# Two transformer blocks on one core: second head pairs, norm rows, first cross-attention scores and a dispatch moved

## The chip, the cores and the metric

The kernel runs on one core of a Trainium2 chip. A core has five engines, each with its own instruction queue: TensorE (PE, matrix products and transpositions, written to PSUM), VectorE (DVE), ScalarE (ACT), GpSimd (POOL) and SyncE (SP, which issues most of the DMA transfers). PSUM has eight banks of 128 x 512 values in float32. Times are microseconds on the device, from a median of several runs; the profile is of one execution.

## The reference

Two transformer blocks follow each other on x of shape (2, 1024, 256), with 16 heads of 16. Block 0 adds self-attention, then cross-attention to 64 context rows, then a mixture of 8 experts of which every row takes two. Block 1 adds self-attention, cross-attention to the same 64 rows (a mask adds 0 or -10000 to the scores), then a dense feed-forward layer. Each step is normed first.

```python
# block 0
q = ln(x);  x = x + mha(q, q, sa)                 # softmax(q k' / 4) v per head
x = x + mha(ln(x), ln(ctx), ca)                   # 64 keys
h = ln(x);  vals, idx = top_k(h @ rw.T + rb, 2)
gates = softmax(vals)
x = x + sum_k gates[k] * (gelu(h @ fc1[idx[k]].T + b1) @ fc2[idx[k]].T + b2)
# block 1
q, k, v = split(ln(x) @ qkv.T);  x = x + softmax(q k' / 4) v @ sa_proj.T
bias = (1 - mask) * -10000
x = x + softmax(ln(x) @ q_w.T (ctx @ k_w.T)' / 4 + bias) (ctx @ v_w.T) @ ca_proj.T
x = x + gelu(ln(x) @ fc1.T + b1) @ fc2.T + b2
```

## The kernel before

The 2048 rows of x lie in SBUF (x_sb, 16 tiles of 128 rows) and are worked on in four units of 512 rows, numbered 0 to 3: batch b = 0 or 1, and half qh = 0 or 1 of its queries.

**Cells.** Each block's self-attention is cut into 128 cells. A cell computes four tiles of 128 x 512 transposed scores (line L969), which ACT turns into exponentials (L947, tile pt_s) and PE multiplies with the values (L1024); ten cells ahead (LEAD = 10) the scores of other four tiles are computed for their row maxima, which DVE reduces (L937). The planner counts 3.3 us for a cell (CELL). From cell 118 on no maxima are left: a flag, maxima[0], turns False. The flag also says which engine helps: helper() is POOL while it is True and DVE afterwards.

**Fillers.** Everything else is a generator (a task) whose yields tell the planner what has been issued: a positive yield is PE time, a negative one is a wait in microseconds before the task may go on. In the cells a wait counts at least one whole cell. A light task advances once a cell by rank; others fill what PE time is left. After the last cell `Stream.rest` plays the tasks that remain, by rank, on a planned clock on which waits count as they are written. What comes out is a fixed order of instructions on each engine, which the engines then run in that order.

**Self-attention's end.** A unit has four groups of four heads, eight cells each (h = 4 * unit + g). When a group's parts are summed (L1037 on POOL, or DVE after cell 118), `finish` sends rows and sums out through DRAM (L538, L539); at the second group of a pair it gathers them (L543), inverts the sums (L554), sends them back (turn_out, L558), spreads them over partitions (spread_out, L562) and divides (L568); each step has its own cell. For a unit's second pair (g == 3, that is h = 3, 7, 11, 15) the projection of the unit (L492, tile ot_s) follows, added to x by DVE (L500). The very last pair of groups goes by L880, L886, L894 and L901 instead.

**Cross-attention of a unit.** Statistics (L398, L399) and inverse roots (L381 to L389, fourteen small operations) of the norm, its rows (xn_c, L412) and their transpositions (L424); the queries (L1295); the scores in `weigh` (L1337, on the tiles q_c and kbd), whose row maxima DVE reduces from PSUM (L1345, tile mx_c); maxima split in two parts (L1358, L1359) and transposed (L1364); scores again, transposed, with the maxima subtracted (L1374, L1380), exponentials (L1385), value products (L1434) and sums (L1444), reciprocals (L1453), division (L1459, L1466) and the projection (L492, tile q_c). In `weigh` the sixteen heads are two groups g of eight; the four rows r of a group are pairs of heads, with 32 of the 128 partitions each. Units 0 and 1 start while maxima[0] is True and go by a finer plan (the `whole` path), units 2 and 3 by the list of steps in the diff. In block 1 each score tile begins with a product that writes the mask (L1324).

**Dispatch of a unit (block 0).** Norm again (st_m, root_m, rows xd_m L1568, transpositions L424), router products (L1581), the top two (L1604 to L1613, the tile hot_m), counts (L1621 to L1642), places and gates (L1647 to L1668), and eight scatters of rows into a DRAM buffer sorted by expert (POOL, L1676). When dispatch 1 has counted, `find(2)` looks up which experts have full tiles (L1689 to L1802); then rows (xs, L1856) and expert weights (L1864) are loaded. An expert slot of 256 rows transposes xs (L1926), turns who and gates (L1932 to L1949), and runs both layers (L1961, L1992) before its results are scattered (L2007). Later slots wait for dispatches 2 and 3. Slots run on after the cells of block 0 and beside the beginning of block 1.

**Block 1's end.** After its cells, the feed-forward layers of units (L2145, L2157) run, with cross-attention of units 2 and 3 between.

PSUM banks come from a list of free ones, in the order in which they were given back; a product waits for whoever used the bank before.

Of the kernel before, what the change touches and what calls it, by code (L numbers as in the profile page):

```python
# [235 lines left out]
def two_blocks(  # L236
# [27 lines left out]
    def bank():  # L264


        i = free.pop(0)
        return i, banks[:, i, :]
# [10 lines left out]
    weights = {}  # L279
# [58 lines left out]
    def choice(layer, pool):  # L338
        for b in range(1 + layer):
            chosen[layer].append(pool.tile([P, 2, P], F32R, name=f"chosen{layer}{b}"))  # L340
# [26 lines left out]
    maxima = [True]  # L367
# [23 lines left out]
    def statistics(src, nt, tag, pool=small, each=False, engine=None):  # L391


        st = pool.tile([P, 8, 6], F32, tag="st", name=f"st_{tag}", bufs=4)
        mv = pool.tile([P, 8, 2], F32, tag="mv", name=f"mv_{tag}", bufs=6)
        rs = pool.tile([P, 8], F32, tag="rs", name=f"rs_{tag}", bufs=6)
        for t in range(nt):
            nc.vector.bn_stats(st[:, t, :], src(t))  # L398
            nc.vector.bn_aggr(mv[:, t, :], st[:, t, :])  # L399
            if each or t % 2 == 1:  # L400
                yield -1.2
        inverse_roots(rs[:, :nt], mv[:, :nt, 1], tag, pool, engine or helper())
        yield -3.4 if engine is None else -4.4
        return mv, rs

    def center(src, pair, held, tag, pool=small):
# [174 lines left out]
    def self_attention(layer, tail, heads, arrive, extra, when_ready, beside=None):  # L581
# [259 lines left out]
        def finish(h, cell):  # L841


            b, qh, g = h // 8, h // 4 % 2, h % 4
            if g == 0:
                ot[b, qh] = opool.tile([P, 2, 512], F32, tag="ot", name=f"ot_{names}{b}{qh}")
            if layer == 0 and h >= 8 * B - 2:

                if g == 3:
                    stream.add(  # L850
                        side_by_side([acc.pop(h - 1), acc.pop(h)], ot[b, qh][:, 1, :]), 2.0,
                        mark="compact", rank=80,
                    )
                    project(b, qh, ["compact"])
                return
            if g % 2 == 0:
                sm = small.tile([P, 32], F32, tag="sums", name=f"sums_{names}{h}")
                sums[g // 2] = next_heads(), sm
            n, sm = sums[g // 2]
            dst = ot[b, qh][:, g // 2, :]  # L860
            send(acc.pop(h), n, g % 2, sm)
            if g % 2 == 1:
                by = opool.tile([P, 512], F32, tag="by", name=f"by_{names}{h}", bufs=1)
                gather(n, dst)
                slow = maxima[0]
                at_cell(cell + 1, lambda: invert(n, sm))
                at_cell(cell + 1 + slow, lambda: turn_out(n, sm))
                at_cell(cell + 2 + slow, lambda: spread_out(n, by))

                late = 3 + 2 * slow  # L870
                at_cell(cell + late, lambda: divide(dst, by))
                if g == 3:
                    at_cell(cell + late + 1, lambda: project(b, qh))
# [434 lines left out]
    def weigh(layer, b, pool, w, name, held):  # L1308
# [7 lines left out]
        mx = pool.tile([P, 2, 4, 4, 2], F32, tag="mxc", name=f"mx_{name}")  # L1316
        turned_mx = []

        def scores(g, n, t0=0, nt=4):

            got = [(r, *bank()) for r in (2 * n, 2 * n + 1)]
            for r, _, p in got if layer == 1 else ():
                at = slice(32 * r, 32 * r + 1)
                nc.tensor.matmul(  # L1324
                    p[:, : nt * P].rearrange("p (c k) -> p c k", k=SK),
                    lhsT=ones[at, :].bitcast(F32R),
                    rhs=mask_f[at, b * SK : (b + 1) * SK]
                    .bitcast(F32R)
                    .unsqueeze(1)
                    .to_broadcast([1, 2 * nt, SK]),  # L1330
                    start=True,
                    stop=False,
                )
            for t in range(nt):
                for r, _, p in got:
                    rows = slice(32 * r, 32 * r + 32)
                    nc.tensor.matmul(  # L1337
                        p[:, t * P : (t + 1) * P],
                        lhsT=q[rows, g, (t0 + t) * P : (t0 + t + 1) * P],
                        rhs=kbd[rows, g, b].rearrange("p u k -> p (u k)"),  # L1340
                        start=layer == 0,
                        stop=layer == 0 or t == nt - 1,
                    )
            for r, i, p in got:
                nc.vector.tensor_reduce(  # L1345
                    mx[:, g, r, t0 : t0 + nt, :].rearrange("p t u -> p (t u)"),
                    p[:, : nt * P].rearrange("p (c k) -> p c k", k=SK),
                    AX.X, ALU.max, negate=True,
                )
                free.append(i)  # L1350
# [120 lines left out]
        if whole:  # L1471
# [2 lines left out]
            cells = [[] for _ in range(22)]  # L1474
            for k in range(8):
                g, n, half = k // 4, k // 2 % 2, k % 2
                cells[k].append((scores, g, n, 2 * half, 2))
                if k % 4 == 3:
                    cells[k].append((parts, g))
            cells[9].append((largest,))  # L1480
# [14 lines left out]
                elif now is not cells[-1]:  # L1495
                    yield 0.0
            return
        costs = {scores: 1.0 + extra, largest: 0.9, weights: 1.2, undivided: 1.9, division: 0.55}
        rs = range(4)
        for step, *args, wait in (  # L1500
            (scores, 0, 0, None),
            (scores, 0, 1, None),
            (parts, 0, None),
            (scores, 1, 0, None),
            (scores, 1, 1, None),
            (parts, 1, -1.8),
            (largest, -0.8),
            (weights, 0, rs, -1.6),
            (undivided, 0, None),
            (weights, 1, rs, -1.6),  # L1510
            (division, 0, None),
            (undivided, 1, None),
        ):
            step(*args)
            if step in costs:
                yield costs[step]
            if wait:
                yield wait
# [36 lines left out]
    def dispatch_task(unit, pool, counted):  # L1555
# [46 lines left out]
        for k in range(2):  # L1602
# [4 lines left out]
            first = small.tile([P, 4], F32, tag="first", name=f"first_{name}{k}")  # L1607
            nc.vector.tensor_reduce(first, hot, AX.X, ALU.max)
            nc.vector.tensor_tensor(hot, desc_b, first.unsqueeze(2).to_broadcast(shape), ALU.is_equal)
            yield -1.0  # L1610
            if k == 0:
                nc.vector.scalar_tensor_tensor(lg, hot, -3.0e38, lg, ALU.mult, ALU.add)
                nc.vector.tensor_scalar(  # L1613
# [51 lines left out]
        for k in range(2):  # L1665
            mine = small.tile([P, 4, E], F32, tag="mine", name=f"mine_{name}{k}")
            nc.vector.tensor_tensor(mine, hots[k], place.rearrange("p e t -> p t e"), ALU.mult)
            nc.vector.tensor_reduce(at[:, k, :], mine, AX.X, ALU.max)  # L1668
            yield -0.5
        counted()  # L1670

        for t in range(4):
# [133 lines left out]
    class Mixture:  # L1806
# [211 lines left out]
        def find(self, units):  # L2018
# [9 lines left out]

                caps = [self.caps[last], *expert_tiles(f"{units}", (OVER, ANY) if last else (FULL,))]
            yield -0.9  # L2030
            pool = self.epool[1] if self.epool else const
            places = Places()
            yield from places.make(pool, f"{units}", n, had, caps, last)
            self.places.append(places)
# [146 lines left out]
    def block(layer, tail, heads=None, beside=None):  # L2181
# [8 lines left out]
        if layer == 0:  # L2190
            open_pools()
            context_places(0, pools["cpool"])
            choice(0, pools["cpool"])
            bias_out.extend(pools["dpool"].tile([P, D], F32, name=f"bias_out{i}") for i in range(2))
        made, ys, ready = [], [], {}

# [310 lines left out]
```

## Time and profile before

| what | us |
|---|---|
| three runs | 1526.99, 1522.6, 1530.24 |
| median | 1526.99 |
| profiled execution | 1523.92 |
| its span | 1522.0 |
| PE busy in it | 1439.3 |
| DVE busy | 982.7 |
| ACT busy | 919.9 |
| POOL busy | 355.3 |
| mean granted PE clock | 0.986 |

A line of the page reads: engine, busy time, share of the span, instructions. A line of a timeline reads: start, length, engine, line of the kernel, operation, output <- inputs, tile sizes, how many instructions were joined, and in brackets how long the engine had been idle before and what released it. A line of the table of stretches reads: from:to, length, busy time of PE, of its weight loads, of DVE, ACT and POOL (with the number of instructions), granted PE clock, share of the DMA engines' time, GB/s. In the profile, block 0's cells end at 543.8 us and what the rest of block 0 and the beginning of block 1 share follows.

### The profile page before, as it was taken

To read this page: it belongs to the slowest core of one execution; us is meant where nothing else is said; L and a number is where in the kernel's file an instruction comes from. 1 tells how busy PE (TensorE), PEld (TensorE's weight loads), DVE (VectorE), ACT (ScalarE), POOL (GpSimd) and SP (SyncE) were. 2 spreads that over 40 slices of the span, in tenths; PEclk is the share of its full clock that TensorE was granted. 3 is DMA by queue.
4 is the path that set the end of the run, shared out by engine and by line. 5 is a ranking of instruction groups with operands and counts; after the bars stand their busy time and mean duration, and the time that the engine had idled before them with its cause. 6 is when DMAs were issued, how large, how long until landed. Compare 5 with 4: busy or idle time off the path is not lost. (4 is left out here: it accounts for less than half of the span.)

```text
span 1522.0 us, 29849 instructions
## 1 busy us (share of the span) xinstructions
PE 1439.3 (95%) x11172; PEld 830.1 (55%) x11172; DVE 982.7 (65%) x2216; ACT 919.9 (60%) x1797; POOL 355.3 (23%) x488
## 2 busy tenths in 40 slices
PE   6999999999999977999999999999999999999998
PEld 3444444444434445788888664444454454446676
DVE  7867788869778665531115758877886886944210
ACT  3377788777777845323323347877877777783411
POOL 2221234225243122031112023211332322411010
PEclk9899999999999998999999999999999999999999
DMA  8653122111110030666566541132211112000000
GB/s 318 248 217 136 52 70 64 43 47 42 36 51 31 15 115 29 215 240 232 188 203 231 169 150 62 61 108 71 64 50 52 44 36 97 29 10 29 8 14 28
DMA packets 69157, 148.71 MB, mean 98 GB/s; under 512 B 12842, under 2 KB 26668, under 8 KB 68620
## 3 DMA queue, kind: packets, MB, share of 16 engines
q1 hardware_dynamic: 65788, 137.86, 26.6%
q0 software_dynamic: 3216, 8.85, 1.6%
q8 instruction: 91, 1.49, 0.4%
q14 instruction: 62, 0.51, 0.1%
HBM read 94.32 MB, written 51.99 MB: 96 GB/s over the span
## 5 line engine op out<-in xcount | busy, mean ns | idle before, releaser
L937 DVE TENSOR_REDUCE mx_s<-banks 128x1 f32<-128x512 f32 x1024 | 635.4, 683 | 131.2 <-PE banks L969 123.4
L947 ACT ACTIVATE pt_s<-banks 128x512 f32<-128x512 f32 x1024 | 535.2, 603 | 125.9 <-PE banks L969 120.1
L1024 PE MATMUL banks<-pt_s,v_s 128*18 128x512 f32 x2048 | 260.6, 603 | 9.6 <-ACT pt_s L947 5.4
L1037 POOL TENSOR_TENSOR acc_s<-acc_s,part_s 128x512 f32<-128x512 f32 x130 | 166.8, 1283 | 419.5 <-ACT part_s L1036 418.8
L969 PE MATMUL banks<-qb_s,ones 2*128 2x512 f32 x1024 | 200.6, 395 | 0.0
L1992 PE MATMUL banks<-w_slot,h_s 128*128 128x256 f32 x560 | 125.1, 380 | 0.4 <-DVE spread L1004 0.4
L1036 ACT COPY part_s<-banks 128x512 f32<-128x512 f32 x145 | 87.1, 601 | 48.0 <-PE banks L1024 42.6
L1992 PEld LDWEIGHTS banks<-w_slot,h_s 128*128 128x128 f32 x560 | 105.4, 190 | 15.6 <-DVE spread L1004 0.8
L1024 PEld LDWEIGHTS banks<-pt_s,v_s 128*18 128x18 f32 x2048 | 43.5, 97 | 126.8 <-ACT pt_s L947 66.4
L2001 DVE SCALAR_TENSOR_TENSOR ys<-banks,gate,b 128x256 f32<-128x256 f32 x35 | 16.9, 483 | 133.2 <-PE banks L1992 133.2
L969 PEld LDWEIGHTS banks<-qb_s,ones 2*128 2x128 f32 x1024 | 96.6, 186 | 8.9
L1967 ACT ACTIVATE h_s<-banks,w_slot 128x256 f32<-128x256 f32 (+1 forms) x104 | 41.1, 446 | 86.1 <-issue 48.3
L2007 POOL DMA_INDIRECT results<-ys,to x35 | 33.8, 966 | 224.3 <-DVE ys L2001 175.6
L1961 PE MATMUL banks<-xsT,w_slot 128*128 128x256 f32 (+1 forms) x416 | 84.9, 357 | 0.9 <-ACT xsT L431 0.9
L1961 PEld LDWEIGHTS banks<-xsT,w_slot 128*128 128x128 f32 x416 | 70.9, 190 | 12.0 <-issue 2.8
L2145 PE MATMUL banks<-hT_f,w_ff 128*128 128x512 f32 x128 | 57.0, 595 | 0.0
L2157 PE MATMUL banks<-w_ff,h_f 128*128 128x256 f32 x256 | 56.6, 379 | 0.0
L1345 DVE TENSOR_REDUCE mx_c<-banks 128x4 f32<-128x256 f32 (+1 forms) x96 | 44.2, 506 | 17.8 <-PE banks L1337 16.7
L698 PE MATMUL banks<-xT_s,w_att 128*128 128x512 f32 x104 | 50.9, 613 | 3.2 <-ACT pt_s L947 2.4
L1967 ACT ACTIVATE h_s<-banks,spare 128x256 f32<-128x256 f32 (+1 forms) x56 | 21.7, 444 | 51.1 <-PE banks L1961 34.9
L2157 PEld LDWEIGHTS banks<-w_ff,h_f 128*128 128x128 f32 x256 | 48.2, 190 | 7.2 <-issue 1.0
L2148 ACT ACTIVATE h_f<-banks,w_ff 128x512 f32<-128x512 f32 x32 | 21.9, 687 | 48.6 <-PE banks L2145 48.6
(376 smaller groups left out, 2926.8 us busy)
## 6 DMA issues: line engine op xcount, KB each, us to landing
w_slot<-in_ff_w_dram SPq DMA_DIRECT2D x40, 576.0 KB
sorted_rows<-fill SPq DMA_DIRECT2D x36, 520.0 KB
w_slot<-in_ff_w_dram SPq DMA_DIRECT2D x26, 514.0 KB
whole<-acc_s SPq DMA_DIRECT2D x30, 256.0 KB
spare<-in_ff_w_dram SPq DMA_DIRECT2D x14, 514.0 KB
q_parts<-spare SPq DMA_DIRECT2D x13, 512.0 KB
KS<-k_parts SPq DMA_DIRECT2D x12, 512.0 KB
k_parts<-spare SPq DMA_DIRECT2D x10, 512.0 KB
```

The costliest lines, as they stand in the source:

```text
L698: nc.tensor.matmul(p, lhsT=w[:, at + k * D + pair * P : at + k * D + (pair + 1) * P], rhs=xT[b][:, k, blk * 512 : (blk + 1) * 512], start= ...
L937: nc.vector.tensor_reduce(to, sc, AX.X, ALU.max)
L947: nc.scalar.activation(pt, sc, AF.Exp, scale=SCALE)
L969: nc.tensor.matmul(sc, lhsT=lhsT, rhs=rhs, start=now[0] == 1, stop=last)
L1024: nc.tensor.matmul(o[32 * j : 32 * j + VW, :], lhsT=V[b][:, cell % 8, 4 * g + j, :], rhs=exps.pop((cell, j)), start=(cell == cells[0]), st ...
L1036: nc.scalar.copy(part, o)
L1037: helper().tensor_tensor(acc[h], acc[h], part, ALU.add)
L1961: nc.tensor.matmul(ph[:, n, :], lhsT=w[:, at : at + P], rhs=xT[:, k, :], start=(k == 0), stop=(k == 1),)
L1967: nc.scalar.activation(h1[:, f, :rows], ph[:, n, :], AF.Gelu, bias=w[:, W_B1 + f : W_B1 + f + 1])
L1992: nc.tensor.matmul(py, lhsT=h1[:, f, h * P : (h + 1) * P], rhs=w[:, f * D : (f + 1) * D], start=(f == 0), stop=(f == 7),)
L2145: nc.tensor.matmul(ph, lhsT=w1[:, at : at + P], rhs=hT[:, k, :], start=(k == 0), stop=(k == 1))
L2157: nc.tensor.matmul(py[:, n, :], lhsT=h1[:, f, t * P : (t + 1) * P], rhs=w2[:, f * D : (f + 1) * D], start=(f == 0), stop=(f == 7),)
```

## The change

Six edits, in the same program.

1. `statistics` (the norm of cross-attention and of dispatch): where the helper is DVE, the pause after the roots is 0.1 us in place of 3.4 us on the planned clock; where it is POOL in the cells it stays.
2. `finish`: in block 0 the second pair of a unit (g == 3) no longer has the additional cells that `slow` gives: turn_out and spread_out come one cell sooner, divide and project two.
3. `weigh`, list of steps: the scores of all four rows of a group are issued together, in four banks, where they were issued in two steps of two banks; the pauses around them change. The finer path still hands in two rows at a time.
4. `dispatch_task`: behind the cells the pauses after the first hot and after the first mine are left out.
5. `find`: when there is no epool, its tiles come from block 0's dpool in place of const.
6. `block`: sets that pool.

The changed kernel has 4120 instructions in PE's order against 4124 (a joined group counted once), 1338 on DVE against 1356, 458 on POOL against 444: dispatch 1's fourteen root operations are on POOL there.

```diff
         inverse_roots(rs[:, :nt], mv[:, :nt, 1], tag, pool, engine or helper())
-        yield -3.4 if engine is None else -4.4
+        yield -4.4 if engine else -3.4 if maxima[0] else -0.1
         return mv, rs
...
-                slow = maxima[0]
+                slow = maxima[0] and (layer == 1 or g == 1)
                 at_cell(cell + 1, lambda: invert(n, sm))
                 at_cell(cell + 1 + slow, lambda: turn_out(n, sm))
                 at_cell(cell + 2 + slow, lambda: spread_out(n, by))
...
-        def scores(g, n, t0=0, nt=4):
+        def scores(g, rs, t0=0, nt=4):
-            got = [(r, *bank()) for r in (2 * n, 2 * n + 1)]
+            got = [(r, *bank()) for r in rs]
...
-                cells[k].append((scores, g, n, 2 * half, 2))
+                cells[k].append((scores, g, (2 * n, 2 * n + 1), 2 * half, 2))
...
-        costs = {scores: 1.0 + extra, largest: 0.9, weights: 1.2, undivided: 1.9, division: 0.55}
+        costs = {scores: 1.3 + 2 * extra, largest: 0.9, weights: 1.2, undivided: 1.9, division: 0.55}
         rs = range(4)
         for step, *args, wait in (
-            (scores, 0, 0, None),
-            (scores, 0, 1, None),
+            (scores, 0, rs, -1.6),
             (parts, 0, None),
-            (scores, 1, 0, None),
-            (scores, 1, 1, None),
-            (parts, 1, -1.8),
+            (scores, 1, rs, None),
+            (parts, 1, -3.0),
             (largest, -0.8),
...
             nc.vector.tensor_tensor(hot, desc_b, first.unsqueeze(2).to_broadcast(shape), ALU.is_equal)
-            yield -1.0
+            if k == 1 or maxima[0]:
+                yield -1.0
...
             nc.vector.tensor_reduce(at[:, k, :], mine, AX.X, ALU.max)
-            yield -0.5
+            if k == 1 or maxima[0]:
+                yield -0.5
...
-            pool = self.epool[1] if self.epool else const
+            pool = self.epool[1] if self.epool else self.scratch
...
             choice(0, pools["cpool"])
+            mixture.scratch = pools["dpool"]
```

## The prediction

> **What bounds the kernel now.** I read the page first: TensorE (PE) is busy for 95% of the span, and the chain that ended last is mostly PE. So time is gained where PE idles, or where the chain leaves PE. Then I read the table of stretches of 20 us, for where PE is not full around the places that the diff touches, and last PE's and VectorE's (DVE's) own timelines in the emptiest stretch.
>
> ```profile
> PE 1439.3 (95%) x11172; PEld 830.1 (55%) x11172; DVE 982.7 (65%) x2216; ACT 919.9 (60%) x1797; POOL 355.3 (23%) x488
> PE 33%; DVE 4%; ACT 3%; issue 1%; DVEq 0%; ACTq 0%
> ```
> ```profile
> 520.00:540.00 20.00, 19.09 (x195) 8.71 (x187) 8.06 (x25) 17.99 (x38) 0.00 (x0) 1.00 0.00 1
> 540.00:560.00 20.00, 18.63 (x156) 12.69 (x157) 12.95 (x51) 8.36 (x18) 8.38 (x9) 1.00 0.28 89
> 560.00:580.00 20.00, 8.82 (x43) 7.07 (x41) 16.36 (x69) 5.67 (x15) 2.63 (x2) 0.74 0.37 131
> 580.00:600.00 20.00, 16.92 (x112) 10.73 (x114) 10.89 (x45) 9.21 (x15) 3.07 (x4) 0.91 0.04 15
> ```
>
> Columns: stretch, length, busy time of PE, weight loads, DVE, ACT, POOL, then PE's granted clock. Behind block 0's cells (they end at 543.8) PE works only 8.82 of 20 us, at a clock of 0.74, while DVE is busy 16.36: DVE bounds this stretch. In 520 to 540, still cells, ACT is the full one (17.99).
>
> ```profile
> 545.31 1.14 PE L1459 MATMUL banks<-inv_c,picks 128*128 128x128 f32 x8
> 546.38 1.06 PE L1434 MATMUL banks<-pt_c,vbd 128*32 128x512 f32 x8
> 572.56 1.11 PE L424 MATMUL banks<-ident,xn_c 128*128 128x128 f32 x4 [9.35 <-DVE xn_c L412]
> 577.21 1.41 PE L424 MATMUL banks<-ident,xd_m 128*128 128x128 f32 x8 [1.83 <-DVE xd_m L1568]
> 586.26 2.28 PE L1337 MATMUL banks<-kbd,q_c 32*128 32x128 f32 x48
> 595.45 0.66 PE L1364 MATMUL banks<-ident,spread 128*128 128x128 f32 x4 [2.33 <-DVE spread L1359]
> ```
> ```profile
> 564.50 0.16 DVE L381 TENSOR_SCALAR root_c<-mv_c 128x4 f32<-128x4 f32 x1
> 567.16 0.42 DVE L398 BATCH_NORM_STATS2 st_m<-x_sb 128x6 f32<-128x256 f32 x1
> 569.42 0.17 DVE L381 TENSOR_SCALAR root_m<-mv_m 128x4 f32<-128x4 f32 x1
> 572.09 2.33 DVE L412 TENSOR_SCALAR xn_c<-x_sb,mv_c,rs_c 128x256 f32<-128x256 f32 x4
> 576.74 1.38 DVE L1568 TENSOR_SCALAR xd_m<-x_sb,mv_m,rs_m 128x256 f32<-128x256 f32 x4 [0.22 <-issue]
> 587.52 1.29 DVE L1345 TENSOR_REDUCE mx_c<-banks 128x8 f32<-128x512 f32 x2 [0.34 <-PE banks L1337]
> ```
> PE stands 9.35 us for the first rows xn_c. Their roots were done at 567.25, yet the rows start at 572.09: the dispatch norm's statistics and roots (567.16 to 572.1) lie between.
>
> **The change, part by part.**
>
> *Second pairs two cells sooner, with the dispatch behind them.* In block 0, h = 3, 7 and 11 divide and project two cells sooner, and each unit's cross-attention and dispatch follow. In the order of the changed program, unit 2's cross-attention then nearly finishes in the cells, and dispatch 1 writes its rows there. What PE did after 544 and now does before: both count products (0.46 us from 544.85 to 545.31), one division (545.31 to 546.38, 1.07), one value product with its sums (546.38 to 548.25, 1.87) and one expert count (550.83 to 551.22, 0.39), together 3.8 us. Ten cells from 504.0 to 543.8 take 39.8 us, with 36 us of ACT and about 31.5 of PE in them, so 3.8 more of PE fits beside ACT. I take 3.3; the ends are 3.8 and 0 (the cells grow by as much). The last PE work before the gap then ends at E = 563.2 - 3.3 = 559.9. Dispatch 1's roots go from DVE to POOL (14 operations; POOL is busy 2.56 of 20 us from 500 to 520). The eight scatters (549.89 to 559.88) come earlier, and the later first load of sorted rows, issued at 565.40, moves up with its expert search.
>
> The move's queues: the returned row of inverse sums has to be there before POOL divides. For h = 3 it is turned at 201.94, spread at 203.37, divided at 207.50, and PE projects at 216.95; two cells are about 7 us (four of PE's later fillers of two cells each start at 1019.08, 1026.26, 1033.44 and 1040.63), so PE still comes after the divide, by some 2 us. POOL, waiting for that row, holds its accumulator additions (1.28 us each) for about 4 us; SP only sends the row a cell sooner. The 3.3 us that PE idles at 400 to 420 and 1.5 at 420 to 440 sit on the first unit's scores and dispatch, which shift together. I take 0 for the cells before 118, ends -4 and +3.
>
> *Rows right behind their roots.* The gap, worked out from E in the changed DVE order: latency 0.25, addition L500 0.6, two st_m tiles at 0.54 (567.16 to 567.72), two st_c 1.1, fourteen root operations 2.7 with 0.2 behind, two more st_c 1.1, first xd 0.35: PE gets xd at about E + 7.3. One xs transposition of 1.06 fills part, so idle 6.2. The eight xd transpositions take 1.4. Then DVE has the rest of xd (1.0), the c roots (2.75) and a first row (0.58): idle 3.0 until xn_c. Before, the two waits were 9.35 + 1.83 = 11.2; now 9.2. So the dispatch is put ahead of cross-attention's norm, and the idle time is cut in two rather than removed.
>
> *Hots and places without their pauses (behind the cells).* No instruction goes away; DVE runs 14 operations of 0.2 in a row, 2.8 us, beside 1.9 us of L1961 and 0.6 of transpositions. I take 1.3 of idle, against 0.44 + 0.30 before (ends 0.3 and 2).
>
> *First scores, four pairs side by side.* Two pairs, two banks at a time take 0.79 us a step. One record is 0.27 long with two lanes truly overlapping; in a lane one follows after 0.11. The nearest row with four lanes is L1374: eight records in 0.56. So sixteen records of four lanes are 8 x 0.11 = 0.9 in place of 1.6, in two groups 1.3 less. DVE still reduces four tiles at 0.64 (1.29 for two), 2.56, behind each group. In the changed order, a group's parts (L1358, L1359), ten search operations of 0.2 and the second group's reductions precede L1364: 2.56 + 2.0 + 0.4 + 2.56 + 0.6 + 0.4 = 8.5 us, with 4.7 us of PE work beside, so 3.8 to 4.2 idle where 2.33 was. That is the stall that comes next.
>
> Idle in the gap: 6.2 + 3.0 + 1.3 + 4.2 = 14.7, against 9.35 + 1.83 + 0.74 + 2.33 + 0.91 (pt_c at 608.59) = 15.2: -0.5, ends -3 and +3. Half clock was granted from 565.8 to 576.0 and from 596.4 to 599.9, behind idle stretches; four xn_c transpositions took 1.11 there and eight L1961 3.12, against 0.66 and 1.99 elsewhere. I take the same loss, ends -3 and +3.
>
> The Trainium skill ("TensorE: Matmul & The Clock Gate", Why this matters for your kernels) says that an idle stretch above about 3 us brings the half clock back. This trace agrees at 565.8 and shows 2.33 us of idle with it at 596. By the rule, three long stretches in place of one would cost an estimated 2 us more, and my sum would be -6.5.
>
> *Scores elsewhere.* In block 0's unit 2 they sit in cells bound by ACT: 0. In block 1's rest, unit 3's four pairs take from 1415.79 to 1419.49, 3.7 us with mask products; four lanes save 1.3, and DVE's reductions lie beside L2145. Unit 2 I price at 1.0 in its cells (ends 0 and 1.3). Norm 3's rows one step sooner: 0, PE is full (20.00 in 1400 to 1420). Sum -2.3, ends -4 and +1.
>
> The Trainium skill ("TensorEngine Tiling (Array Packing)", PSUM Bottleneck) warns that tiling speeds up TensorE but not the emptying of PSUM. The row 0.64 per tile agrees; by that rule every group waits for its reductions, the scores' 1.3 in the gap and 2.3 in block 1 are worth nothing, and the sum would be -4.9.
>
> *The rest.* Waits at 624.52 and 630.55 (0.8) come off in part: -0.8, ends 0 and -1.7. The beside stage from 640 to 840 is full (PE 20.00 in each stretch): -0.3. The search's pool is only another place in memory: 0.
>
> **Sum:** -3.3 (cells) - 0.5 (idle) - 1.3 (scores in the gap) - 0.8 (later waits) - 0.3 - 2.3 (block 1) = -8.5 us. On the profiled execution, 1523.92 (span 1522.0), that is 1515.4; it lies 3.07 below the median of the runs, 1526.99, on which it is 1518.5. I say 1518. All good ends together give about -23, all bad ones about +14; terms are mostly independent, so 8 in 10 lie within 11 or 12 of the sum.
>
> **The rivals.**
> 1. *The gap only changes shape* (no difference): E comes earlier, but DVE's list is as long as before, 16.36 us in its stretch, and the cells grow by the fillers. What stays is 1.3 + 2.3: -3.6, 1523.4. For it: xn_c comes later in DVE's order than xd. Against it: ACT's cover of 36 us with PE at 31.5.
> 2. *Shorter gap at full clock* (larger gain): the xs transposition lands in mid-gap and splits the idle, so the half clock is granted for one stretch only: -3 more; the clump at 400 to 431 resolves, another -4: -15.5, 1511.5.
> 3. *Slower:* a group takes four of eight banks at once and gives them back only after DVE's 2.56 us; in the cells PE is in order, so the next cell's scores wait. Already with two, 1.25 and 1.75 us rows stand at 516.41 and 517.76 where 0.5 and 0.79 belong. Two groups in each of four units, each losing 2.56: 20.5, less 8.5: +12, 1539. It decides from 1.1 us a group on; above 2.0 a group it is slower by over 0.5%. Against it: outside the cells (two units) other PE work lies behind the group.
> 4. *The change does not do what it says:* the projects wait for the returned sums and start where they did; then the gap's order is as before and only scores count: like rival 1, 1523.
>
> **How the numbers follow.** 0.5% of 1527 is 7.6 us, about what a measurement can tell from no change, so the bound is 1519.4: the forecast lies just beyond it. Chances: forecast 0.48 (1513 to 1522, of which two thirds is faster by over 0.5%), rivals 1 and 4 0.27 (within), rival 2 0.13 (faster), rival 3 0.12 (two thirds of it over 0.5%). Faster 0.32 + 0.13 + 0.05 of good tails in rival 1 = 0.50; slower 0.09; same 0.41. The range: from rival 2's side 1507 to 1529, leaving a tail of 0.05 to 0.1 at each end; the forecast's own is 1513 to 1522.
>
> **What would show it.** Right: the first xd transposition behind the gap is preceded by a wait of 6 us and xn_c's by 3; L1364's wait grows to about 4; PE's last product ahead of the gap ends near 560; sixteen L1337 records take 0.9 us in block 1's rest. Wrong: L969 rows of 1 us or more beside unit 2's scores; POOL's divide of h = 3 coming after PE's project; a half clock through all of E to E + 20; or an xs load that lands after E + 6 and holds PE in order.

## The result and the profile after

The forecast was wrong, in sign and in range: 1518 us (1507 to 1529) was said, and the changed kernel took 1531.76 us (median of 20 runs, 1526.53 to 1538.75) against 1527.01 us of before (20 runs, 1522.6 to 1532.93). The ratio is 1.0029, 95% interval 1.0015 to 1.0043. The profiled execution of after took 1536.07 us, its span is 1534.1 us at a mean granted clock of 0.978 (before: 1523.92, 1522.0 and 0.986). So the profile of after lies 4.3 above its median and that of before 3.1 below: 7.4 of the 12.1 us between the two profiles are chance, and each reading below is tested again in other runs.

The page, the busy times and the shares of the chain:

```profile
PE 1444.0 (94%) x11172; PEld 828.2 (54%) x11172; DVE 975.7 (64%) x2200; ACT 917.4 (60%) x1792; POOL 357.7 (23%) x501
PE 32%; DVE 4%; ACT 3%; DMA 1%; issue 1%; POOL 0%; SPq 0%; DVEq 0%; ACTq 0%; POOLq 0%
```

PE executes as many instructions as before (11172); "DMA 1%" is new in the chain. The stretches that the prediction read, now of after:

```profile
540.00:560.00 20.00, 16.58 (x125) 7.20 (x122) 6.11 (x22) 9.85 (x20) 8.35 (x9) 0.83 0.18 59
560.00:580.00 20.00, 13.29 (x83) 10.33 (x82) 13.09 (x55) 4.55 (x12) 0.00 (x0) 0.97 0.45 160
580.00:600.00 20.00, 15.15 (x59) 9.49 (x60) 12.89 (x64) 11.43 (x20) 4.00 (x4) 0.77 0.02 6
```

Two things stand out. The gap has moved later, into 575 to 586, because the cells' last value products end at 558.6 instead of 544.9. And in 540 to 560 no engine is full: PE 16.58, DVE 6.11, ACT 9.85. PE's timeline there, then ACT's, DVE's and POOL's:

```profile
546.61 0.82 PE L1444 MATMUL banks<-pt_c,picks 128*32 128x128 f32 x18
548.10 0.39 PE L1444 MATMUL banks<-pt_c,picks 128*32 128x128 f32 x2 [0.67 <-issue]
549.51 0.44 PE L1444 MATMUL banks<-pt_c,picks 128*32 128x128 f32 x4 [1.02 <-issue]
550.95 0.38 PE L1444 MATMUL banks<-pt_c,picks 128*32 128x128 f32 x2 [1.00 <-issue]
551.69 0.37 PE L1444 MATMUL banks<-pt_c,picks 128*32 128x128 f32 x1 [0.36 <-issue]
552.39 0.67 PE L1444 MATMUL banks<-pt_c,picks 128*32 128x128 f32 x5 [0.34 <-issue]
```
```profile
552.45 0.59 ACT L1451 COPY q_c<-banks 128x512 f32<-128x512 f32 x1 [6.32 <-remote]
```
```profile
549.56 0.69 DVE L1466 TENSOR_TENSOR q_c<-q_c,banks 128x512 f32<-128x512 f32 x1 [1.53 <-remote]
```
```profile
540.90 1.08 POOL L1676 DMA_INDIRECT sorted_rows<-xd_m,at_m  x1 [28.62 <-DVE mine_m L1666]
...
546.10 0.96 POOL L1676 DMA_INDIRECT sorted_rows<-xd_m,at_m  x1 [0.30 <-issue]
...
549.90 0.96 POOL L1676 DMA_INDIRECT sorted_rows<-xd_m,at_m  x1 [0.30 <-issue]
```

The 32 count products L1444 take 1.2 us when they run on (the kernel `spaced3`, below). Here the last fourteen need from 547.4 to 553.1, a few at a time, with pauses of up to 1 us ahead of which the profile puts only "issue": nothing that it records was missing. ACT and DVE pause too, released by "remote". PE and ACT move again at 552.4, and DVE behind PE. What is going on elsewhere at that time is dispatch 1: its eight scatters run from 540.90 to 550.86, 1.27 us apart, and the slow time lasts from the sixth to 1.5 us behind the last. The same picture stands at dispatch 0 (scatters from 430.59 to 440.70, ACT released at 442.35) and at dispatch 2 (from 598.21 to 608.08, ACT released at 609.75). I call it the stall. It is no full stop. These are the 5 us from the sixth scatter on, in after for dispatches 0, 1 and 2, then in before for dispatches 1 and 2:

```profile
437.30:442.30 5.00, 3.51 (x18) 0.74 (x18) 1.99 (x4) 1.20 (x2) 2.79 (x3) 0.66 0.30 107
547.40:552.40 5.00, 1.60 (x11) 0.62 (x10) 1.25 (x5) 0.00 (x0) 2.85 (x3) 0.92 0.30 107
604.60:609.60 5.00, 1.61 (x23) 1.23 (x22) 2.07 (x3) 0.00 (x0) 2.88 (x3) 1.00 0.30 107
```
```profile
556.40:561.40 5.00, 5.00 (x25) 4.41 (x24) 4.12 (x16) 0.00 (x0) 2.87 (x3) 1.00 0.52 119
602.40:607.40 5.00, 5.00 (x61) 3.05 (x61) 1.83 (x8) 4.27 (x7) 2.84 (x3) 1.00 0.30 107
```

In the stall PE works 1.6 us of 5 at dispatches 1 and 2, and 3.51 at a clock of 0.66 at dispatch 0. In before the scatters of dispatches 1 and 2 follow each other as closely (1.26 to 1.38 us), and PE works all of the 5 us. So an unbroken series is not enough for a stall; what must come together with it is open. A late load of instructions is not it: the profile marks such packets ("instruction"), and in after none starts in 436 to 455, 538.8 to 553 or 599.6 to 610, while ACT goes on at 442.35, 552.45 and 609.75.

Where the time went, by stages (each from the first value product L1024 of one cell to that of another, worked out from the traces; us; "rest" runs from the end of block 0's cells to the first cell of block 1, and the last stage ends with PE's last product):

| kernel | cells 86 to 104 | 104 to 118 | 118 to end | rest | block 1, cells 0 to 16 | 16 to 118 | 118 to end |
|---|---|---|---|---|---|---|---|
| before | 77.0 | 49.3 | 32.4 | 363.3 | 57.3 | 376.2 | 176.0 |
| after | 84.3 | 48.7 | 39.0 | 362.3 | 58.8 | 376.2 | 173.9 |

The two stages that grew by 7.3 and 6.6 us hold dispatch 0 and dispatch 1. In the rest and at the end the change gave 1.0 and 2.1.

### The profile page after: what moved, and what is told of

It reads as the page before. It is cut to its first block, busy times and chain, and to the rows that moved or that the text cites. A ratio compares the mean times of both kernels' runs of the same rounds, so it can differ in the third digit from the quotient of the medians.

```text
span 1534.1 us, 29834 instructions
## 1 busy us (share of the span) xinstructions
PE 1444.0 (94%) x11172; PEld 828.2 (54%) x11172; DVE 975.7 (64%) x2200; ACT 917.4 (60%) x1792; POOL 357.7 (23%) x501
## 3 DMA queue, kind: packets, MB, share of 16 engines
q1 hardware_dynamic: 65788, 137.86, 26.5%
## 5 line engine op out<-in xcount | busy, mean ns | idle before, releaser
L1024 PE MATMUL banks<-pt_s,v_s 128*18 128x512 f32 x2048 | 261.7, 610 | 10.0 <-ACT pt_s L947 5.2
L1037 POOL TENSOR_TENSOR acc_s<-acc_s,part_s 128x512 f32<-128x512 f32 x129 | 165.7, 1285 | 415.0 <-ACT part_s L1036 414.5
L969 PE MATMUL banks<-qb_s,ones 2*128 2x512 f32 x1024 | 201.3, 397 | 0.0
L1992 PE MATMUL banks<-w_slot,h_s 128*128 128x256 f32 x560 | 130.5, 390 | 2.4 <-issue 1.9
L1024 PEld LDWEIGHTS banks<-pt_s,v_s 128*18 128x18 f32 x2048 | 43.9, 97 | 129.4 <-ACT pt_s L947 66.6
L2001 DVE SCALAR_TENSOR_TENSOR ys<-banks,gate,b 128x256 f32<-128x256 f32 x35 | 16.9, 483 | 138.4 <-PE banks L1992 135.5
L969 PEld LDWEIGHTS banks<-qb_s,ones 2*128 2x128 f32 x1024 | 96.7, 187 | 8.7
```

The source lines that it names most:

```text
L969: nc.tensor.matmul(sc, lhsT=lhsT, rhs=rhs, start=now[0] == 1, stop=last)
L1024: nc.tensor.matmul(o[32 * j : 32 * j + VW, :], lhsT=V[b][:, cell % 8, 4 * g + j, :], rhs=exps.pop((cell, j)), start=(cell == cells[0]), st ...
L1037: helper().tensor_tensor(acc[h], acc[h], part, ALU.add)
L1992: nc.tensor.matmul(py, lhsT=h1[:, f, h * P : (h + 1) * P], rhs=w[:, f * D : (f + 1) * D], start=(f == 0), stop=(f == 7),)
```

## The experiments

Kernels that were measured together ran on one chip, beside runs of before. There were five chips, here A to E; that of the first 20 runs is not on record. Two numbers go with each ratio below: *lower clock* is the span times (1 - mean granted clock), the mean over all runs of that kernel, so what the runs below full clock can have cost; *work* is the span less that. A run's clock is listed to 0.001, which is 1.5 us, and the means are over 5 to 35 runs.

| kernel | chip | ratio to before, 95% | lower clock | work |
|---|---|---|---|---|
| before | A, B, C, D, E | 1 | 21.5, 20.6, 21.4, 20.6, 20.1 | 1504.4, 1498.8, 1505.6, 1504.4, 1504.2 |
| after (first) | not on record | 1.0029, 1.0015 to 1.0043 | 27.0 | 1502.8 |
| after (again) | A | 1.0003, 0.9989 to 1.0017 | 24.7 | 1502.5 |
| after (again3) | C | 1.0014, 1.0000 to 1.0029 | 27.7 | 1501.6 |
| after (again4) | D | 1.0012, 0.9994 to 1.0030 | 24.9 | 1501.9 |
| second_alone | A | 0.9999, 0.9983 to 1.0015 | 27.6 | 1499.3 |
| without_second | A | 0.9991, 0.9971 to 1.0011 | 24.5 | 1500.8 |
| scores_alone | A | 1.0032, 1.0017 to 1.0047 | 29.9 | 1501.6 |
| norm_alone | B | 1.0028, 1.0018 to 1.0038 | 26.5 | 1497.5 |
| without_norm | D | 1.0092, 1.0068 to 1.0116 | 31.5 | 1506.8 |
| spaced | B | 0.9910, 0.9897 to 0.9924 | 16.9 | 1490.4 |
| spaced3 | C | 0.9976, 0.9963 to 0.9990 | 23.1 | 1501.3 |
| warm | B | 0.9930, 0.9912 to 0.9948 | 17.6 | 1491.4 |
| warm3 | C | 1.0035, 1.0020 to 1.0049 | 26.7 | 1505.2 |
| spaced_all | D | 0.9930, 0.9910 to 0.9950 | 20.2 | 1494.5 |
| spaced_all5 | E | 0.9953, 0.9935 to 0.9972 | 22.3 | 1494.0 |
| before_spaced | D | 0.9973, 0.9961 to 0.9985 | 20.9 | 1499.9 |
| before_spaced5 | E | 0.9972, 0.9958 to 0.9986 | 20.6 | 1499.3 |

Read by these columns, after's work is 1.9 to 4.0 us below before's on A, C and D, and its lower clock, 3.2 to 6.3 us above, takes that back.

### The change again, and its edits alone

The first question was which edit costs the time: the second pairs' earlier steps (edit 2), which put dispatch 1 into the cells, or the four banks of the scores (edit 3). `again` is the changed kernel; `second_alone` is before with edits 2, 5 and 6; `scores_alone` is before with edit 3; `without_second` is after with

```diff
-                slow = maxima[0] and (layer == 1 or g == 1)
+                slow = maxima[0]
```

> The changed kernel once more. The profile shows PE, ACT and DVE standing together for 3 to 7 us inside three series of eight scatters (437 to 442, 547 to 552, 604 to 609), which the kernel before shows in none of its series. Theory S (the scatters' new places cause it): the same three stalls again within a few cells, and a ratio near 1.003. Theory R (they come by chance, whatever the kernel): no stall or others elsewhere, a profiled time under 1530, and the median's loss of about 4.4 us has another cause.

> The kernel before with the second pairs two cells sooner (and the search's other pool) alone. Theory S: the loss is here, ratio 1.002 to 1.005 (3 to 8 us slower), with the stalls in the scatters of dispatch 0 and 1. Theory G (the gap behind the cells is what lost, by norms and scores there): 0.996 to 0.999, 2 to 6 us faster, as more PE work sits in the cells.

> The changed kernel with the second pairs where they were. Theory S: 0.995 to 0.999, 2 to 7 us faster than before, from norm rows and scores. Theory G: 1.002 to 1.006, the gap behind the cells costs as in the changed kernel or more.

> The kernel before with four rows of scores side by side alone. By my prediction's price 1.3 us in the gap and 2.3 in block 1: ratio 0.9976. If the emptying of PSUM bounds both places: 1.000, and if the four banks hold up the cells: 1.002 or more.

Measured on chip A: 1.0003, 0.9999, 0.9991 and 1.0032. Neither edit by itself is the answer. Edit 2 alone costs nothing in sum, the change without it is no better than the change with it (the intervals overlap), and `scores_alone` loses in a way of its own. But whether dispatch 0 stalls goes with edit 2: `second_alone` has that stall (430.5 to 435.5: PE 3.40 of 5 us at a clock of 0.72). In before, dispatch 0's series is broken by other work of POOL, here a division L568 between the fourth and the fifth:

```profile
441.34 0.96 POOL L1676 DMA_INDIRECT sorted_rows<-xd_m,at_m  x1 [0.30 <-issue]
442.32 1.28 POOL L568 TENSOR_TENSOR ot_s<-ot_s,by_s 128x512 f32<-128x512 f32 x1
443.77 1.00 POOL L1676 DMA_INDIRECT sorted_rows<-xd_m,at_m  x1 [0.17 <-DVE mx_s L937]
```

In after the dispatch is earlier, the division waits for its row until 448.79, and the eight scatters follow each other without a break; ACT's row shows the stall behind them:

```profile
437.20 0.96 POOL L1676 DMA_INDIRECT sorted_rows<-xd_m,at_m  x1 [0.31 <-issue]
438.47 0.96 POOL L1676 DMA_INDIRECT sorted_rows<-xd_m,at_m  x1 [0.30 <-issue]
439.74 0.96 POOL L1676 DMA_INDIRECT sorted_rows<-xd_m,at_m  x1 [0.31 <-issue]
448.79 1.27 POOL L568 TENSOR_TENSOR ot_s<-ot_s,by_s 128x512 f32<-128x512 f32 x1 [8.09 <-DMA by_s<-turns]
```
```profile
442.35 1.08 ACT L947 ACTIVATE pt_s<-banks 128x512 f32<-128x512 f32 x2 [3.67 <-remote]
```

`without_second` keeps the break and has no stall at dispatch 0 (cells 86 to 104 take 76.3 us, against 80.1 in `again`). Its dispatch 1, which without edit 2 still begins 2.7 us ahead of the cells' end, is unbroken and stalls (544.5 to 549.5: PE 2.25 of 5 us).

`scores_alone` loses, and shows the mechanism of the prediction's rival 3. PE's and DVE's timelines of it:

```profile
511.83 2.96 PE L1337 MATMUL banks<-kbd,q_c 32*128 32x128 f32 x30 [0.31 <-DVE mx_c L1345]
514.42 0.79 PE L969 MATMUL banks<-QS03h,KS 32*128 32x512 f32 x3
```
```profile
511.09 2.48 DVE L1345 TENSOR_REDUCE mx_c<-banks 128x8 f32<-128x512 f32 x4
...
515.09 2.48 DVE L1345 TENSOR_REDUCE mx_c<-banks 128x8 f32<-128x512 f32 x4
```

The second group of unit 2 needs 2.96 us, because its banks come free one by one as DVE reduces the first group; the cell's scores L969 queue behind it. The stage from 118 to the end takes 39.1 us in place of 32.4. That is not all: its rest takes 371.5 us (before's profiles have 361.6 to 370.3), and at 634.75 PE has waited 7.15 us for the second slot's rows. The two costs were not separated. Two cells earlier, as in the full change, this collision is gone (32.2 to 32.4 in the kernels without a stall, below).

### Fewer scatters in a row; a busy PE in the gap; the norm alone

The next theory: the unbroken series stalls all engines. `spaced` is after with a write ahead of each scatter of dispatch 1 (an identity, so that the output stays). In POOL's order four of the eight writes come well before the first scatter; the other four stand between the last scatters, and can wait for the scatter that read the rows before:

```diff
+                if unit == 1:
+                    same = xd[:, t, :D]
+                    nc.gpsimd.tensor_scalar(same, same, 1.0, None, ALU.mult)
```

Rival: PE loses its full clock in the gap. `warm` is after with 26 products of the identity with itself, into a bank that nobody reads, ahead of dispatch 2's transpositions. `norm_alone` is before with edit 1, and `before_again` is before.

> The changed kernel; POOL multiplies the rows of dispatch 1 by one ahead of each scatter, so that only the first four of its eight scatters follow each other at 1.27 us, and each of the last four waits for an earlier one to land. Theory S (PE, ACT and DVE stand still in the second half of an unbroken series, 5.0 us from 547.4 to 552.4 and again from 539.4 to 544.4 in the second profile): no stall longer than 1 us in dispatch 1, and 3 to 6 us less than the changed kernel, a ratio to before of 0.997 to 1.000. Theory D (the stall belongs to PE's run of 32 short products and to nothing else): the stall stays at L1444, ratio 1.000 to 1.003. If the stall goes and the time does not, what follows it (DVE's list behind the cells) takes the time back.

> The changed kernel with 26 products of the identity (some 5.5 us) on PE ahead of the first rows xd behind the cells, where it idles 6.8 us. Theory C (the half clock costs in the gap): no half clock from E + 4 on; eight transpositions there take 1.4 in place of 1.97, four 0.66 in place of 1.11, L1579 1.9 in place of 2.97: 2 us less than the changed kernel. If DVE bounds the gap, PE runs faster and waits longer: within 0.5 us of the changed kernel, and the waits for xn_c and chosen_m grow by what the products save.

> The kernel before with norm's rows right behind their roots alone. By my prediction's working the gap's idle time is cut in two, 9.2 for 11.2: ratio 0.9985 to 1.000. If the dispatch's rows ahead of cross-attention's delay the queries and scores: 1.001 to 1.004.

> The kernel before once more, for a second profile. If the clock is granted by chance of the window, the half clock's stretches and the span differ between the two profiles by several us with PE's idle time in each stage equal to 0.5 us; series of scatters show no stall of PE.

Measured on chip B: 0.9910, 0.9930, 1.0028, and 1521.17 us for before (1521.66 in the median). `spaced` and `warm` won by more than the forecast's 0.994, so this tells nothing between the theories: `warm`, whose scatters are as unbroken as after's, has no stall in its profile either. Nor has any profile of this chip. In work, `spaced` and `warm` lie 1.0 apart (1490.4 and 1491.4): where nothing stalls, the break gave no more than that. `norm_alone` is a loss that no stall explains. Dispatch 1's rows (L1568, 1.38 us) are now ahead of the reductions that PE waits for:

```profile
514.42 1.38 DVE L1568 TENSOR_SCALAR xd_m<-x_sb,mv_m,rs_m 128x256 f32<-128x256 f32 x4
515.72 2.47 DVE L1345 TENSOR_REDUCE mx_c<-banks 128x8 f32<-128x512 f32 x4
```
```profile
516.46 1.09 PE L969 MATMUL banks<-QS03h,KS 32*128 32x512 f32 x2 [0.96 <-DVE mx_c L1345]
```

The stretch from 520 to 540 has a granted clock of 0.83 (1.00 in before), and the last stage of the cells takes 37.0 us. In the table its work is 1.3 less than before's and its lower clock 5.9 more.

### The same on another chip

To separate chip and kernel, `again3`, `warm3` and `spaced3` repeat after, `warm` and `spaced`; `before3` is before.

> The changed kernel a third time, beside spaced and warm on one chip. In the last call warm, with its scatters unbroken, showed no stall of PE in dispatch 1 and ran at 0.993, so the stall may belong to the chip or the hour. Theory H (a stall that some chips have and some have not): where the profile shows stalls of PE in the series of scatters the ratio is 1.000 to 1.003, where it shows none 0.993 to 0.996, which is what my working without a stall gave (0.9944). Theory W (warm's products were worth it): no stall and still above 0.997.

> Theory H: within 2 us of the changed kernel of this call, both with stalls or both without. Theory W: 6 us or more below it.

> Theory S with H: where the changed kernel of this call shows the stall in dispatch 1, 4 to 6 us below it and no stall there; where it shows none, within 2 us.

> The kernel before, for its profile on this chip. Theory H: where the changed kernel stalls, this one shows waits of ACT, DVE or PE of 1 us and more in the later half of its series of scatters too, and its span lies near 1526; where not, near 1519 and none.

Measured on chip C: 1.0014, 1.0035, 0.9976; before took 1527.02 us in the profiled run. Here `warm` gains nothing: keeping PE busy does not pay. That its gain on B was the chip's fits this, but is not shown, as after itself did not run on B. `spaced3` is 0.4% below `again3`, with intervals that do not touch. One run holds its own control: in `spaced3` dispatch 1, the only one that is spaced, has no stall (118 to the end takes 32.4 us, against 38.7 in `again3`), while dispatches 0 and 2 of the same execution still have theirs (86 to 104 takes 81.3). PE's timelines at dispatch 1, `again3` and then `spaced3`:

```profile
544.72 0.68 PE L1444 MATMUL banks<-pt_c,picks 128*32 128x128 f32 x6 [0.77 <-issue]
```
```profile
539.55 1.20 PE L1444 MATMUL banks<-pt_c,picks 128*32 128x128 f32 x32
```

`before3` has it too, at dispatch 2 (scatters from 596.30 to 606.14, PE 3.21 of the 5 us from 602.7 on), so before is not free of it on such a chip; in before's first profile the same products run on. PE's timeline:

```profile
606.26 0.42 PE L1444 MATMUL banks<-pt_c,picks 128*32 128x128 f32 x3 [0.79 <-issue]
607.67 0.60 PE L1444 MATMUL banks<-pt_c,picks 128*32 128x128 f32 x10 [0.99 <-issue]
```

### All four dispatches spaced, in both kernels

`spaced_all` is after, `before_spaced` before, each with the write ahead of the scatters in all four dispatches (`if unit == 1` becomes `if True`). `without_norm` is after without edit 1.

> The changed kernel; ahead of each scatter of every dispatch POOL multiplies the rows by one, so that a series of eight is broken after the fourth. Theory S: on a chip where the changed kernel stalls, the stalls in dispatch 0 (5 us at 435 in the last call) and dispatch 2 (5 to 7 us at 599) go as that of dispatch 1 went: 0.990 to 0.996 to before, 8 to 15 us below the changed kernel; on a chip without stalls equal to it within 2 us, 0.990 to 0.994. If only dispatch 1's place mattered: 0.997 to 0.999 on a chip with stalls.

> The kernel before with the same multiplications. Its series in dispatch 0 is already broken by two additions of POOL, those of dispatches 1 and 2 are not. Theory S: on a chip with stalls 3 to 8 us faster than before, 0.995 to 0.998, on a chip without 1.000. If the stalls of the kernel before cost nothing: 1.000 on both.

> The changed kernel on this call's chip, to know which kind of chip it is. With stalls of PE in its series of scatters 1.000 to 1.003; without 0.991 to 0.995.

> The changed kernel without norm's rows right behind their roots. By my prediction's working (waits of 11.2 us in place of 9.2) 0.5 to 2 us slower than the changed kernel of this call. If the rows' order costs in the changed kernel as it did alone (1.0028): 3 to 5 us faster.

> The changed kernel with the last four of every eight scatters behind a landing, a second time and on another chip if there is one. Theory (the unbroken series stalls PE, ACT and DVE; without it the change is worth about what was forecast): 0.992 to 0.995 of before, as 0.993 on the chip before, and about 6 us below the spaced kernel of before beside it, whether or not this chip shows the stalls at all. Rival (the 0.993 was that chip's, or six runs' luck): 0.997 or more.

> Before with the same spacing. Theory: 0.997 where the chip shows stalls in the kernel of before, 1.000 on a chip that shows none (the wait itself costs nothing, POOL has room). Rival (the wait gains or loses something of its own): away from both by over 0.002.

Measured on chip D: 0.9930, 0.9973, 1.0012 and 1.0092; on chip E 0.9953 and 0.9972. `spaced_all` beats both kernels, at 1517.33 and 1519.27 us against 1527.2 and 1525.97. POOL's timeline of it, with the writes between the scatters (which are L1679 here), and the stretch around dispatch 0 of after and then of `spaced_all`:

```profile
430.27 0.96 POOL L1679 DMA_INDIRECT sorted_rows<-xd_m,at_m  x1 [0.30 <-issue]
431.26 0.89 POOL L1676 TENSOR_SCALAR xd_m<-xd_m 128x256 f32<-128x256 f32 x1
432.68 2.48 POOL L1676 TENSOR_SCALAR xd_m<-xd_m 128x256 f32<-128x256 f32 x3 [0.54 <-DMA sorted_rows<-xd_m,at_m]
435.32 1.03 POOL L1679 DMA_INDIRECT sorted_rows<-xd_m,at_m  x1 [0.16 <-POOL xd_m L1676]
```
```profile
430.00:450.00 20.00, 17.21 (x120) 5.96 (x116) 8.45 (x17) 10.51 (x20) 9.18 (x9) 0.74 0.27 94
```
```profile
430.00:450.00 20.00, 18.14 (x152) 7.31 (x148) 11.02 (x21) 13.57 (x26) 12.01 (x12) 0.91 0.22 72
```

The fifth scatter starts 5.05 us after the fourth here, where the pitch was 1.27; at dispatches 1 and 2 the last scatters stand up to 2.9 apart. Most of the break is POOL's writes, 0.8 to 0.9 us each; the wait for a landing is 0.54. No profile of a spaced dispatch has a stall. By stages:

| kernel | cells 86 to 104 | 118 to end | rest | block 1, 118 to end |
|---|---|---|---|---|
| again4 (D) | 81.8 | 39.0 | 362.5 | 173.9 |
| spaced_all (D) | 77.6 | 32.3 | 357.3 | 173.9 |
| before_spaced (D) | 76.6 | 32.4 | 361.3 | 176.0 |
| spaced_all5 (E) | 75.2 | 32.2 | 356.1 | 173.9 |
| before_spaced5 (E) | 76.7 | 32.3 | 363.6 | 176.0 |
| before_again (B) | 77.1 | 32.4 | 361.6 | 175.9 |
| spaced (B) | 75.2 | 32.2 | 353.9 | 173.9 |

With the stalls out of both kernels, the change is worth 0.9930 / 0.9973 = 0.9957 on D and 0.9953 / 0.9972 = 0.9981 on E: 6.6 and 2.9 us, where about 6 was expected on E. On D the two intervals do not touch, on E they overlap. In work it is 5.4 and 5.3 (1499.9 - 1494.5 and 1499.3 - 1494.0). What the spacing itself gives is 4.5 to 4.9 us of work in before (1504.4 and 1504.2 to 1499.9 and 1499.3) and 7.4 in after (1501.9 to 1494.5, on D), where it also takes the lower clock from 24.9 to 20.2. On E the profiles of both spaced kernels show no stall either. On B, where no profile shows stalls, before unspaced has 1498.8 of work: about what spacing brings it down to on D and E. That fits the stall as the whole of the spacing's gain, but before without spacing was not profiled on D or E.

`without_norm` surprised me most: edit 1, which loses 0.28% alone, is worth 0.8% inside the change (1.0092 against 1.0012), on one chip and in six runs. PE's timeline of it shows where:

```profile
628.81 1.97 PE L1926 MATMUL banks<-ident,xs 128*128 128x128 f32 x8 [8.99 <-DMA xs<-sorted_rows]
```

PE stands 9 us for the second slot's rows. The slot's loads stand behind dispatch 2, whose first scatter is at 595.23 here and at 592.58 in `again4`, where the same transposition at 625.37 has no wait ahead of it. How 2.7 us grow to 9 was not followed further; `scores_alone` has the same wait.

## Why the prediction was wrong, step by step

**The step that failed** is the move of the scatters. The prediction wrote that the eight scatters "come earlier", and for the cells before 118 "I take 0", since unit 0's dispatch would only shift. It looked at what waits for the scatters, not at what runs beside them or at what lay between them. The trace of before shows POOL's L568 and L1037 between dispatch 0's scatters, and dispatch 1's from 549.89 on, behind the cells, with PE busy for nearly all of the time. In after dispatch 0's series is unbroken, dispatch 1's lies in the cells, and both stall, as does dispatch 2. Why before's unbroken dispatches 1 and 2 do not stall in its first profile is not known, so that the new place beside the cells' work is what does it is argued, not shown. What it cost in the profile is 7.3 and 6.6 us in the two stages. In the table, breaking the series frees 7.4 us of work and 4.7 of lower clock in after on D, against 4.5 and nothing in before. The difference is 7.6 us, and more than half of it is clock, for which the prediction took "the same loss". Of the 13 us between the forecast's -8.5 and the measured +4.8 that is the larger part; the change without stalls gave -2.9 to -6.6 in place of -8.5, and the rest is scatter between chips (+0.5 to +4.8 for the same two kernels). That the stall would appear was not readable from the profile of before, which shows none; no row of it bounded the price, and the range had no room for it.

**Cells, -3.3: right in kind, 2.0 in size.** Where nothing stalls, the last stage takes 32.2 to 32.4 us with the additional fillers, as before with 32.4, so they fit. The reason given was misread: from 504.0 to 543.8 the trace of before has PE busy for 37.80 us and ACT for 33.46, not 31.5 and 36. The last PE work ahead of the gap ends at 560.1 in `spaced_all` (forecast 559.9), but that the times agree is in part luck, as block 0's cells end 1.1 us earlier in that execution. From the end of the cells it is 16.3 us (16.3 on E, too) against 18.3 in before: 2.0 are gained. PE has a new wait there, 1.35 us for a division of DVE (L1466) at 546.71.

**The gap: right in shape.** The waits, PE's timeline of `spaced_all`:

```profile
567.35 1.97 PE L424 MATMUL banks<-ident,xd_m 128*128 128x128 f32 x8 [6.84 <-DVE xd_m L1566]
572.33 1.11 PE L424 MATMUL banks<-ident,xn_c 128*128 128x128 f32 x4 [3.01 <-DVE xn_c L412]
581.52 0.41 PE L1640 MATMUL banks<-chosen_m,tri 128*128 128x32 f32 x2 [0.68 <-DVE chosen_m L1620]
598.97 0.81 PE L1364 MATMUL banks<-ident,spread 128*128 128x128 f32 x4 [4.41 <-DVE spread L1359]
```

Said were 6.2, 3.0, 1.3 (0.98 with the 0.30 at 582.23) and 4.2. The terms that the prediction lists for the first one add up to 6.8 us from the last product to xd, not to 7.3; measured are 7.3 (560.08 to 567.35), so its total was right and its list short. In after itself the second is 2.11 and the last 1.98; the stall at 604 to 609 took the place of part of the last:

```profile
604.66 0.50 PE L1337 MATMUL banks<-kbd,q_c 32*128 32x128 f32 x6
607.54 1.05 PE L1337 MATMUL banks<-kbd,q_c 32*128 32x128 f32 x15 [2.39 <-DVE mx_c L1345]
609.60 1.23 PE L1337 MATMUL banks<-kbd,q_c 32*128 32x128 f32 x11 [1.00 <-issue]
```

Rest and gap together gave 4.0 us on D (357.3 against 361.3, both spaced) and 7.5 on E (356.1 against 363.6), where -3.3, -0.5, -1.3, -0.8 and -0.3, together -6.2, were said.

**Scores in four banks.** In the gap, -1.3 was too much: in `spaced_all` the first group takes 1.17 us and the second 1.57 (0.9 was said for each), together 2.74, where four steps of 0.79 took 3.16: -0.4. In block 1's rest the size was near, -2.1 for -2.3; ten of thirteen profiles with the edit have 173.9 us in the last stage (the others 175.5, 175.5 and 178.7), the seven without it 175.7 to 177.6. The timeline of after:

```profile
1427.48 1.06 PE L1337 MATMUL banks<-kbd,q_c 32*128 32x128 f32 x32
1428.48 1.99 PE L2157 MATMUL banks<-w_ff,h_f 128*128 128x256 f32 x8
1430.74 1.06 PE L1337 MATMUL banks<-kbd,q_c 32*128 32x128 f32 x32
```

Between the groups lies a layer's product, 1.99, which covers most of DVE's 2.48 for a group's reductions. The rule quoted from the Trainium skill ("TensorEngine Tiling (Array Packing)", PSUM Bottleneck), that tiling does not empty PSUM faster, agrees with both: DVE takes 2.48 in `scores_alone` as well. There PE's second group waits for it (2.96), here not: what it costs depends on what is issued between.

**Half clock, "the same loss": wrong with stalls, near without.** Lower clock is 24.7 to 27.7 us in after against 20.1 to 21.5 of before, and 20.2 and 22.3 in the spaced kernel against 20.9 and 20.6. The skill's warning of idle stretches above 3 us ("TensorE: Matmul & The Clock Gate", Why this matters for your kernels), by which I would have taken 2 us more for the gap, was nearer; but on D the excess went with the stalls (24.9 to 20.2), while the gap kept its three waits. Its remedy of a busy array did not pay here: `warm3` keeps PE at work through most of the first wait and is 1.0035 against 1.0014. On B, PE's timeline of `warm`:

```profile
557.95 5.97 PE L1575 MATMUL banks<-ident 128*128 128x128 f32 x52
564.92 1.40 PE L424 MATMUL banks<-ident,xd_m 128*128 128x128 f32 x8 [1.00 <-DVE xd_m L1566]
569.09 1.09 PE L424 MATMUL banks<-ident,xn_c 128*128 128x128 f32 x4 [2.77 <-DVE xn_c L412]
```

The transpositions of xd take 1.40 in place of 1.97, but xn_c comes when DVE has it, and that wait grows.

**The rivals.** Rival 3 (four banks in the cells) has its mechanism in `scores_alone`, but not in the full change, whose stage from 118 on is clean without stalls. Rivals 1 and 4 missed: the gap did change and the steps did move. Rival 2's 1511.5 is near the chip without stalls (1508.5 and 1509.88 for its two variants of after); why B's kernels gain more than those on D and E is not explained.

## What to carry to other kernels

When a change moves DMA issues, ask what stands between them and what runs beside them, not only who waits for them: here breaks in the series of indirect scatters, one of which was there by accident, were worth 12 us to the changed kernel on chip D, more than the change itself (2.9 to 6.6). If several engines pause together with "issue" or "remote" as releasers, look for a series of transfers at that time, and break it by something that the queue can afford. And price an edit within the set: edit 1 lost 0.28% alone and saved 0.8% in company.

## What the runs showed of the hardware

While GpSimd sent eight indirect scatters, 1.27 us apart without a break, PE, ACT and DVE lost most of their work together, from the sixth on until 1.5 to 1.7 us behind the last, about 5 us each time (in after at 437, 547 and 604). The scatters themselves were issued at an even pace. With breaks after the fourth no profile shows it (D, E and dispatch 1 on C). It was there in every profile of after (the first, A, C and D), and in none of B's four. An unbroken series can also pass without it: in before's first profile PE works 5.00 of 5 us beside it, twice. What decides, why B is free of it, and what the engines wait for, is open: the records name no releaser. Each run listed has a span and a clock, so each was recorded; whether the recording has a part in the stall is open too.
